# The same ends, spreading, maxima and first steps, with the conv's x added by VectorE behind the maxima

## The chip, the core and the metric

The kernel runs on one core of a Trainium2 chip. The core has five engines that work side by side, each through its own list of instructions in order: TensorE (PE in the profile; its weight loads are PEld), VectorE (DVE), ScalarE (ACT), GpSimd (POOL) and SyncE (SP), which here only issues DMAs. Engines wait for one another by semaphores. The metric is the time of one execution on the device, in microseconds (us); the median of several runs is compared. Everything is computed in float32.

## The reference

The input x has 16 images of 192 channels and 56 x 56 = 3136 pixels. Three layers of one kind and one of another follow, each with a residual:

```
x = x + rwkv(gn(x))          # layers 0, 1, 2
x = x + graph_conv(gn(x))    # layer 3

gn: per image and group of 6 channels, mean and variance over the group and all pixels

rwkv(x):                      # tokens t = the 3136 pixels, row by row
  k = x Wk,  v = x Wv,  r = x Wr
  forward and backward over the tokens, each with a decay per channel:
     y_t = (P_t + exp(u + k_t) v_t) / (Q_t + exp(u + k_t))
     P, Q: decaying sums of exp(k) v and exp(k) over the tokens before
  h = sigmoid(r) * (y_forward + y_backward) / 2
  h = layernorm over the 192 channels of each token
  return h Wo

graph_conv(x):
  m = max over the pixels 2 rows up, 2 rows down, 2 columns left and right (cyclic), minus x, and at least 0
  y = [x, m] (384 channels) times a matrix to 192 channels, + bias, batch norm
  return gelu(y)
```

## The kernel before

**Tiles.** The 16 images make 8 pairs. A pair's 2 x 192 channels lie as tiles of 128 partitions x 3 x 448 tokens: part j = 0 holds image A's first 128 channels, j = 2 image B's, and j = 1 the last 64 of both (A's in partitions 0-63, B's in 64-127; the code calls these halves LO and HI). A layer's tokens are cut into 7 chunks of 448 (8 image rows). Tiles live in a fixed set of slots in SBUF that go round a free list, results of matmuls in seven PSUM banks. What a layer hands to the next goes through DRAM.

**Runs and units.** A run is one layer of one pair. A forward unit "A" is one chunk of an RWKV layer: keys and values (`a_keys`, `a_values`), exp, forward scans (`a_q`, `a_p`), the bonus term (`a_den`, `a_num`) and y. A backward unit "B" is one chunk from last to first: gate r (`b_gate`, `b_exp`), backward scans (`b_q`, `b_p`, VectorE, L875), denominators (`b_den`, VectorE, L890), their inversion by Ln and Exp on ScalarE (`invert`, L975 and L978), numerators (`b_num`, L890), the mix of both directions with the gate (`b_mix`, nine GpSimd ops, L1031-L1033), squares (`b_squares`, ScalarE, L1040), sums over channels by matmuls with ones (`b_sums`, tile st, L1047-L1049), 1/deviation by `b_rs1` (ScalarE, L1055), `b_rs2` (PE) and `b_rs3` (ScalarE Ln and Exp, L1063 and L1065), the spreading of that row to all partitions by matmuls with a picking matrix (`b_spread`, tile rsb, L1071), scaling (`b_scale`, VectorE, L1076), output product (`b_out`, tile ops) and residual (`b_x`, L1089), then the sums that the next GroupNorm needs (`chunk_stats`, L734 and L735). A unit "C" is one chunk of the conv: maxima over rows and columns (`c_rows` L1114-L1116, `c_columns` L1125-L1129, VectorE), products of x and of the maxima (`c_product`, tile cv), gelu (`c_gelu`, ScalarE, L1150, with a load of its table before and of the usual one behind, L1155), and x added (`c_add`, GpSimd, L1159), then stores.

**GroupNorm** is folded into the weights: `norm_sums`, `norm_var` (mean nm, m2 = mean squared at L751, variance, rstd), `norm_fold` (weights times rstd on ScalarE, L770), and a mean column behind the first chunk (L765) that gives the bias through the same product.

**Order.** Even and odd pairs make two streams. A planner (L1207-L1242) lays out steps: a B turn has seven chunks, 6 to 0; the first stands alone (`backward_alone`), the other six stand beside six chunks of the other stream's next layer. There are 24 turns: 17 beside A, where chunk 5 runs in `both_a_first` and chunks 4 to 0 in `both_a`, and 7 beside C (`both_c`, 42 steps); what is left of the forward runs alone (`forward_a`, `forward_c`). At the end pair 6's last conv chunk and, after the step `neither`, pair 7's seven conv chunks stand alone. Within a step every engine's order is that in which the step's function calls the pieces, written out by hand; a piece enters its instructions at the end of the queues of all engines that it uses. `late` tells which B chunk still has which of its last stages to come; `gap()` marks places where a piece of the next run's norm may be put.

At the start, statistics of the first pair's input are counted for all seven chunks (`count`, ScalarE), before the first norm. A flag of checks on the values is reduced and written after the last chunk (L1758-L1763).

Of the kernel before, what the change touches and what calls it, by code (L numbers as in the profile page):

```python
# [473 lines left out]
def fast_path(ctx: ExitStack, tc: tile.TileContext, flag, x, wproj, wfold, wcfold, wconst, wgroup, sums, picks, vecs, out):  # L474
# [237 lines left out]
    class Run:  # L712
        def __init__(self, pr, l, stats, src=None, first=None):
            self.pr, self.l, self.stats, self.src = pr, l, stats, src
            self.xa, self.xb, self.xz = {}, {}, {}
            if first is not None:
                self.xa[0] = first
            self.begun, self.before = False, None
            self.bias, self.ps = {}, {}
            self.ek, self.ekv, self.h, self.den, self.sg, self.rs = {}, {}, {}, {}, {}, {}  # L720
            self.m, self.ml, self.q, self.p = {}, {}, {}, {}
            self.done = set()
# [23 lines left out]
    def norm_var(run):  # L746
# [4 lines left out]
        V.tensor_mul(m2, nm, nm)  # L751
# [10 lines left out]
        mean_column(run, run.xa[0])  # L762
# [47 lines left out]
    def load_weights(run):  # L810
        kv = wpool.tile([P, 2, FCOLS], F32, tag="kv", name=name("wkv"))
        if run.l == NLAYERS:
            nc.sync.dma_start(kv, wcfold)
            run.weights = kv, None
        else:
            nc.sync.dma_start(kv, wfold[run.l, :, 0:2, :])
            r = wpool.tile([P, 1, FCOLS], F32, tag="r", name=name("wr"))
            nc.sync.dma_start(r, wfold[run.l, :, 2:3, :])
            run.weights = kv, r
        load_ahead(("C" if run.l == NLAYERS else "A", run, 0))  # L820
# [14 lines left out]
    def load_ahead(unit):  # L835
# [7 lines left out]
        if kind == "C" and c not in run.xb:  # L843

            ring = run.xb[c] = Slot("m")
            nc.sync.dma_start(ring.t[:, :, 0:SHIFT], run.src[(c - 1) % NL][:, :, L - SHIFT : L])
            nc.sync.dma_start(ring.t[:, :, L - SHIFT : L], run.src[(c + 1) % NL][:, :, 0:SHIFT])
# [213 lines left out]
    def b_rs3(run, c):  # L1061
        rs, st = run.rs[c], run.ps["st"]
        S.activation(rs[HI, :], st[HI, :L], AF.Ln, bias=eps4[HI, :])  # L1063
        release(st)
        S.activation(rs[HI, :], rs[HI, :], AF.Exp, scale=-0.5)  # L1065

    def b_spread(run, c):
        rs = run.rs.pop(c)
        ps = run.ps["rsb"] = banks("rsb")
        for j, rows in ((0, slice(64, 96)), (2, slice(96, P)), (1, HI)):  # L1070
            PE.matmul(ps[j][:, :L], pick[rows, j, :], rs[rows, :], start=True, stop=True)  # L1071
# [36 lines left out]
    def c_rows(run, c):  # L1108
# [3 lines left out]
        if c == 0:  # L1112
            mean_column(run, m)
        V.tensor_max(m.t[:, :, SHIFT:E], xt[:, :, 0 : E - SHIFT], xt[:, :, 2 * SHIFT : L])  # L1114
        V.tensor_max(m.t[:, :, 0:SHIFT], m.t[:, :, 0:SHIFT], xt[:, :, SHIFT : 2 * SHIFT])
        V.tensor_max(m.t[:, :, E:L], xt[:, :, E - SHIFT : E], m.t[:, :, E:L])  # L1116

    def c_columns(run, c):
# [3 lines left out]
        for j in ORDER:  # L1122
            xr = xt[:, j, :].rearrange("p (r w) -> p r w", w=W)
            mr = ml.t[:, j, :].rearrange("p (r w) -> p r w", w=W)
            V.tensor_max(mr[:, :, 2 : W - 2], xr[:, :, 0 : W - 4], xr[:, :, 4:W])  # L1125
            V.tensor_max(mr[:, :, 0:2], xr[:, :, W - 2 : W], xr[:, :, 2:4])
            V.tensor_max(mr[:, :, W - 2 : W], xr[:, :, W - 4 : W - 2], xr[:, :, 0:2])
        V.tensor_max(ml.t, ml.t, xt)
        V.tensor_max(m, m, ml.t)  # L1129

    def c_product(run, c, half):
        n = L + 1 if c == 0 else L
# [7 lines left out]
    def c_gelu(run, c, more):  # L1140
        g, ps = run.ml[c], run.ps["c"]
        if c == 0:
# [14 lines left out]
    def c_add(run, c):  # L1157
        xs, g = run.xa.pop(c), run.ml.pop(c)
        G.tensor_add(g.t, g.t, xs.t)  # L1159
# [5 lines left out]
    def c_end(run, c, more):  # L1165
        c_gelu(run, c, more)
        c_add(run, c)

# [25 lines left out]
    for pr in range(npairs):  # L1194
        runs = [Run(pr, 0, None)]
        for l in range(NLAYERS):
            runs[-1].follow = Run(pr, l + 1, None)
            runs[-1].follow.before = runs[-1]
            runs[-1].dst = [dram.tile([P, 3, L], F32, tag=f"x{pr}_{l}_{c}", name=name("xd")) for c in range(NL)]
            runs.append(runs[-1].follow)  # L1200
# [11 lines left out]
    while ready[turn] is not None:  # L1212
# [16 lines left out]
        if len(streams) == 1 or ready[other] is None:  # L1229
# [8 lines left out]
            else:  # L1238
                ready[turn] = None
            steps += [[None, None, []]] + [[None, u, []] for u in units]  # L1240
# [139 lines left out]
    def both_a_first(b, a, nback, nfront, loads):  # L1380
# [7 lines left out]
        b_q(*b)  # L1388
        b_sigmoid(*b)
        b_p(*b)  # L1390
        b_den(*b)
        invert(b[0].ek[b[1]])
        b_num(*b)
# [3 lines left out]
        a_ekv(*a)  # L1397
# [4 lines left out]
        b_rs1(*l)  # L1402
        if nback is not None:
            b_exp(*nback[1:])
        a_q(*a)
        b_rs2(*l)
        b_rs3(*l)
        keys(nfront)
        a_p(*a)
        spread_and_scale(l)  # L1410
# [4 lines left out]
        b_sums(*b)  # L1415
        a_den(*a)
# [10 lines left out]
    def both_c(b, a, nback, nfront, loads):  # L1427
# [51 lines left out]
        gap()  # L1479
        b_num(*b)  # L1480
        b_sigmoid(*b)
        b_mix(*b)
        if ended:
            c_add(*ended)
# [33 lines left out]
    def forward_a(a, nback, nfront, nkeys, z):  # L1518
# [14 lines left out]
        if l:  # L1533
# [3 lines left out]
            b_spread(*l)  # L1537
            a_den(*a)
            invert(den())
            sum_up()  # L1540
            a_ekv(*a)
# [66 lines left out]
    def forward_c(a, nback, nfront):  # L1608
# [5 lines left out]
        if h and ahead and nfront[0] == "A":  # L1614
# [16 lines left out]
            return  # L1631
        c_product(*a, 0)
        c_rows(*a)
        c_columns(*a)
# [12 lines left out]
        c_end(*a, nfront is not None and nfront[0] == "C")  # L1647
# [23 lines left out]
    def backward_alone(b, nback, nfront):  # L1671
# [8 lines left out]
        invert(b[0].ek[b[1]])  # L1680
        b_sigmoid(*b)
        b_p(*b)
        gap(G)
# [22 lines left out]

    with tc.manual_schedule(engines={PE.engine, V.engine, S.engine, G.engine, nc.sync.engine}):
        S.preload_act_table_set(TABLES)
        first = chains[0][0]
        for c in range(NL):  # L1710
            load_ahead(("Z", first, c))
        for c in range(NL):
            count([(first, c, j) for j in ORDER], 3)
        for i, (b, f, z) in enumerate(steps):
# [32 lines left out]
            elif f:  # L1747
                forward_c(f[1:], nback, nfront)
# [7 lines left out]


    least = small.tile([P, 1], F32, tag="p2", name="fleast")  # L1758
    V.tensor_reduce(least, ok, mybir.AxisListType.X, ALU.min)
    ps = bank("psok")  # L1760

    PE.matmul(ps[0:32, 0:1], ones[:, 0, :], least, start=True, stop=True)
    V.tensor_scalar(flag, ps[0:1, 0:1], (P - 0.5) / C, None, ALU.is_lt)  # L1763
# [44 lines left out]
def _lay_out(inputs):  # L1808
# [24 lines left out]
    picks[64, 0, :] = picks[64, 1, 0:64] = picks[96, 1, 64:P] = picks[96, 2, :] = 1.0  # L1833
# [22 lines left out]
```

## Time and profile before

| what | us |
|---|---|
| median of 3 runs | 5122.39 |
| lowest and highest of them | 5105.55, 5124.11 |
| profiled execution, its own time | 5118.31 |
| its span (first to last instruction) | 5116.5 |
| busy: TensorE / VectorE | 4664.1 / 4769.5 |
| busy: ScalarE / GpSimd | 3690.8 / 2898.8 |
| mean granted TensorE clock | 0.95 of full |
| a turn beside A, from one turn's L890 `b_den` to the next turn's | about 179 |
| of it: step of chunk 5 / 4 / each of 3, 2, 1 | 30.5 or 32.1 / 25.7 / 23.6 |

A row of a group or of single instructions reads: line of the code, engine, operation, out<-in by tile names, shape; in brackets the idle time before it and what ended it. A row of a table by stretch reads: stretch and its length, then busy time of PE, PEld, DVE, ACT and POOL with the number of instructions, the granted clock, the share of DMA and GB/s.

### The profile page before, as it was taken

The page shows a single profiled execution, that of the slowest core. Times are in us where ns is not written, and L with a number is a line of the kernel's source. Part 1 is how long each engine was busy: PE and PEld are TensorE (multiplying, and loading weights), DVE is VectorE, ACT ScalarE, POOL GpSimd, SP SyncE. Part 2 cuts the span into 40 slices and gives each one's busy share as a digit, 9 for nine tenths or more (in the row PEclk, how much of TensorE's full clock was granted, in tenths as well). Part 3 has the DMA queues.
Part 4 walks back from the last instruction along what each step waited for, and adds up shares of the span by engine and source line. Part 5 has one row for each costly group of instructions (what it writes and reads, how often), then busy time and mean ns, then how long its engine had stood idle before and what let it go on. Part 6 is the DMA issues. An engine that isn't in the chain of part 4 may idle for free.

```text
span 5116.5 us, 51926 instructions
## 1 busy us (share of the span) xinstructions
PE 4664.1 (91%) x15542; PEld 1474.9 (29%) x15542; DVE 4769.5 (93%) x6275; ACT 3690.8 (72%) x7163; POOL 2898.8 (57%) x2247
## 2 busy tenths in 40 slices
PE   7899999999898999999989899999989999999897
PEld 3222222222222223222323222322222322223222
DVE  5999999998999999999899999999989999999995
ACT  6777777776767777777776777777767577777672
POOL 1656656654455666565455556666635466566562
PEclk9999999999899999999999999999999999999998
DMA  6122222234242222223424222222343322222233
GB/s 173 60 84 82 80 87 84 79 103 144 79 129 88 85 76 89 78 76 121 138 89 126 79 83 72 89 89 78 114 124 113 103 65 84 78 71 89 74 100 119
DMA packets 314276, 482.49 MB, mean 94 GB/s; under 512 B 66432, under 2 KB 306688, under 8 KB 313984
## 3 DMA queue, kind: packets, MB, share of 16 engines
q1 hardware_dynamic: 312832, 477.59, 29.2%
q8 instruction: 126, 2.06, 0.2%
q10 hardware_dynamic: 1152, 1.48, 0.1%
q14 instruction: 166, 1.36, 0.1%
HBM read 324.83 MB, written 154.14 MB: 94 GB/s over the span
## 4 chain that ended last, share of the span: by engine, by line
PE 35%; DVE 23%; POOL 18%; ACT 17%; issue 4%; DMA 2%; SPq 1%; POOLq 0%; DVEq 0%; ACTq 0%
POOL p L1033 6%; POOL p L1032 6%; POOL ekv L1031 5%; DVE p L875 5%; DVE q L875 4%; PE st L1049 3%; DVE q L890 2%; ACT sg L1003 2%; PE st L1059 2%; ACT sg L978 2%; ACT ek L978 2%; PE rsb L1071 2%; PE r L598 2%; PE r L605 2%; PE r L600 2%
## 5 line engine op out<-in xcount | busy, mean ns | idle before, releaser
L875 DVE TENSOR_TENSOR_SCAN q<-fdecays,ek 128x449 f32<-128x449 f32 (+1 forms) x1008 | 1023.5, 1068 | 12.8 <-ACT ek L920 10.3
L875 DVE TENSOR_TENSOR_SCAN p<-fdecays,ekv 128x449 f32<-128x449 f32 (+1 forms) x1008 | 1020.1, 1064 | 15.1 <-ACT ek L884 14.9
L1031 POOL TENSOR_TENSOR ekv<-ekv,ek 128x448 f32<-128x448 f32 x504 | 609.6, 1210 | 607.6 <-ACT ek L978 284.3
L982 POOL TENSOR_TENSOR p<-p,q 128x1344 f32<-128x1344 f32 x168 | 512.2, 3049 | 749.8 <-ACT q L978 468.6
L1033 POOL TENSOR_TENSOR p<-p,sg 128x448 f32<-128x448 f32 x504 | 616.8, 1224 | 83.4 <-ACT sg L978 34.0
L1032 POOL TENSOR_TENSOR p<-p,ekv 128x448 f32<-128x448 f32 x504 | 602.3, 1195 | 39.5
L886 POOL COPY ekv<-p 128x3 f32<-128x3 f32 x282 | 243.8, 864 | 567.0 <-DVE p L875 544.4
L920 ACT ACTIVATE ek<-k,k 128x448 f32<-128x448 f32 x504 | 297.1, 632 | 285.6 <-PE k L601 229.2
L1040 ACT ACTIVATE ek<-p 128x448 f32<-128x448 f32 x504 | 286.3, 572 | 231.2 <-POOL p L1033 230.8
L735 ACT ACTIVATE fjunk<-x 128x448 f32<-128x448 f32 x672 | 387.7, 577 | 37.6 <-DVE x L1089 11.1
L1071 PE MATMUL rsb<-rs,fpicks 32*128 32x448 f32 (+1 forms) x1008 | 355.3, 619 | 43.1 <-ACT rs L1065 43.1
L1076 DVE TENSOR_TENSOR p<-p,rsb 128x448 f32<-128x448 f32 x504 | 281.4, 611 | 103.7 <-PE rsb L1071 103.7
L890 DVE SCALAR_TENSOR_TENSOR ek<-ek,fcc,q 128x896 f32<-128x896 f32 x336 | 377.7, 1163 | 0.0
L734 ACT ACTIVATE fjunk<-x 128x448 f32<-128x448 f32 x600 | 343.5, 572 | 13.6
L1089 DVE SCALAR_TENSOR_TENSOR x<-ops,fwob,x 128x448 f32<-128x448 f32 x504 | 313.2, 669 | 29.5 <-PE ops L601 16.2
L890 DVE SCALAR_TENSOR_TENSOR q<-ek,fcc,q 128x896 f32<-128x896 f32 x336 | 334.7, 1035 | 6.3 <-ACT cvb L954 4.6
L940 DVE SCALAR_TENSOR_TENSOR ekv<-v,v,ek 128x448 f32<-128x448 f32 x504 | 312.3, 671 | 15.3 <-PE v L601 10.9
L890 DVE SCALAR_TENSOR_TENSOR ekv<-ekv,fcc,p 128x896 f32<-128x896 f32 x336 | 321.7, 997 | 0.0
L996 ACT ACTIVATE sg<-r,r 128x448 f32<-128x448 f32 x504 | 312.4, 626 | 10.2 <-PE r L607 8.3
L890 DVE SCALAR_TENSOR_TENSOR p<-ekv,fcc,p 128x896 f32<-128x896 f32 x336 | 293.6, 913 | 3.8 <-POOL ekv L886 1.7
L975 ACT ACTIVATE q<-q 128x1344 f32<-128x1344 f32 x168 | 221.5, 1318 | 96.9 <-DVE q L890 87.8
L598 PE MATMUL ops<-p,fwo 128*128 128x448 f32 x336 | 206.1, 700 | 84.5 <-DVE p L1076 84.5
(235 smaller groups left out, 11485.2 us busy)
## 6 DMA issues: line engine op xcount, KB each, us to landing
x<-xd SPq DMA_DIRECT2D x240, 672.0 KB, 5.3
xd<-x SPq DMA_DIRECT2D x168, 672.0 KB, 3.9
x<-in_x_dram SPq DMA_DIRECT2D x320, 224.0 KB, 4.5
x<-in_x_dram SPq DMA_DIRECT2D x320, 112.0 KB, 4.4
out_dram<-ml SPq DMA_DIRECT2D x112, 224.0 KB, 2.3
m<-xd SPq DMA_DIRECT2D x112, 168.0 KB, 5.2
wkv<-in_wfold_dram SPq DMA_DIRECT2D x24, 640.0 KB, 5.5
out_dram<-ml SPq DMA_DIRECT2D x112, 112.0 KB, 2.3
```

Source lines behind the costliest of these rows:

```text
L734: S.activation(junk, xt[:, j, :], AF.Identity, accum_out=stats[:, 0, j, c : c + 1])
L735: S.activation(junk, xt[:, j, :], AF.Square, accum_out=stats[:, 1, j, c : c + 1])
L875: V.tensor_tensor_scan(out, dec[:, column(j)].to_broadcast([P, L if first else L + 1]), e, 0.0, ALU.mult, ALU.add)
L890: by_channel(lambda js, i: V.scalar_tensor_tensor(dst.t[:, js, :], e.t[:, js, :], cc[:, i : i + 1], state.t[:, js, :], ALU.mult, ALU.add))
L940: V.scalar_tensor_tensor(e.t[:, j, :], ps[j][:, 0:L], b[:, j, :], run.ek[c].t[:, j, :], ALU.add, ALU.mult)
L982: G.tensor_mul(run.h[c].t, run.h[c].t, den.t)
L996: S.activation(sg.t[:, j, :], ps[j][:, 0:L], AF.Exp, bias=b[:, j, :], scale=-1.0, accum_out=run.chk[:, at : at + 1])
L1031: G.tensor_mul(y.t[:, j, :], y.t[:, j, :], den.t[:, j, :])
L1032: G.tensor_add(h.t[:, j, :], h.t[:, j, :], y.t[:, j, :])
L1033: G.tensor_mul(h.t[:, j, :], h.t[:, j, :], sg.t[:, j, :])
L1071: PE.matmul(ps[j][:, :L], pick[rows, j, :], rs[rows, :], start=True, stop=True)
L1089: V.scalar_tensor_tensor(xj, ps[j][:, 0:L], wob[:, column(j)], xj, ALU.add, ALU.add, accum_out=run.new[:, 0, j, c : c + 1] if c == 0 else ...
```

## The change

- Start: the first run's sums come from one VectorE reduction per chunk; ScalarE only squares.
- `norm_var`: m2 is made from the sums in PSUM and nm, instead of nm times nm.
- Spreading: `b_rs3` writes the same row with one more Exp into the lower 64 partitions too, and `b_spread` takes j = 1 from rows 0-63 instead of 64-127 (`picks` accordingly).
- Maxima: the two border operations of `c_rows` become one, the nine of `c_columns` three over all j.
- `both_a_first`: another order, in which the next B chunk's scans are done in this step, and 1/deviation and spreading of the chunk before follow right behind its sums.
- `both_c`: x is added to the gelu of the chunk before by VectorE, behind the maxima, not by GpSimd behind `b_mix`. That holds for five of a turn's seven chunks; the others stay on GpSimd.
- `forward_a`: `a_ekv` stands before `a_den`. `backward_alone`: a piece of the norm stands before the sigmoid and `b_p`, not behind.
- End: beside pair 6's last conv chunk the last B chunk's rest comes first, pair 7's last norm and maxima of two of its chunks are put there; pair 7's conv takes its chunks in the order 3, 4, 5, 2, 6, 1, 0, the flag is written before the last of them, and that one's gelu, addition (VectorE) and store go part by part.

The diff, cut to its core:

```diff
@@ Run, norm_var
+            self.c0 = 0
...
-        V.tensor_mul(m2, nm, nm)
+        V.scalar_tensor_tensor(m2, m[:, :, 0:1], -1.0 / T, nm, ALU.mult, ALU.mult)
...
-        mean_column(run, run.xa[0])
+        mean_column(run, run.xa[run.c0])
+        if run.c0 in run.m:
+            mean_column(run, run.m[run.c0])
@@ b_rs3, b_spread
+        S.activation(rs[LO, :], rs[HI, :], AF.Exp, scale=-0.5)
         S.activation(rs[HI, :], rs[HI, :], AF.Exp, scale=-0.5)
...
-        for j, rows in ((0, slice(64, 96)), (2, slice(96, P)), (1, HI)):
+        for j, rows in ((0, slice(64, 96)), (2, slice(96, P)), (1, LO)):
@@ c_rows, c_columns
-        V.tensor_max(m.t[:, :, 0:SHIFT], m.t[:, :, 0:SHIFT], xt[:, :, SHIFT : 2 * SHIFT])
-        V.tensor_max(m.t[:, :, E:L], xt[:, :, E - SHIFT : E], m.t[:, :, E:L])
+        mq, xq = (t.rearrange("p j (q k) -> p j q k", k=SHIFT) for t in (m.t, xt))
+        V.tensor_max(mq[:, :, ::3], mq[:, :, ::3], xq[:, :, 1:3])
...
-        for j in ORDER:
...
-            V.tensor_max(mr[:, :, 2 : W - 2], xr[:, :, 0 : W - 4], xr[:, :, 4:W])
-            V.tensor_max(mr[:, :, 0:2], xr[:, :, W - 2 : W], xr[:, :, 2:4])
-            V.tensor_max(mr[:, :, W - 2 : W], xr[:, :, W - 4 : W - 2], xr[:, :, 0:2])
+        xr, mr = (t.rearrange("p j (r w) -> p j r w", w=W) for t in (xt, ml.t))
+        V.tensor_max(mr[:, :, :, 2 : W - 2], xr[:, :, :, 0 : W - 4], xr[:, :, :, 4:W])
+        V.tensor_max(mr[:, :, :, 0:2], xr[:, :, :, W - 2 : W], xr[:, :, :, 2:4])
+        V.tensor_max(mr[:, :, :, W - 2 : W], xr[:, :, :, W - 4 : W - 2], xr[:, :, :, 0:2])
@@ c_add, c_end_in_parts
-    def c_add(run, c):
+    def c_add(run, c, eng=G):
         xs, g = run.xa.pop(c), run.ml.pop(c)
-        G.tensor_add(g.t, g.t, xs.t)
+        eng.tensor_add(g.t, g.t, xs.t)
...
+    def c_end_in_parts(run, c):
...
+        for j in ORDER:
+            S.activation(
+                g.t[:, j, :], ps[j][:, 0:L], AF.Gelu, bias=run.bias["c"][:, j, :], scale=conv_inv[:, column(j)]
+            )
+            release(ps[j])
+            V.tensor_add(g.t[:, j, :], g.t[:, j, :], xs.t[:, j, :])
+            if j == 1:
+                nc.sync.dma_start(out[b0, P:C, cols], g.t[LO, 1, :])
+                nc.sync.dma_start(out[b1, P:C, cols], g.t[HI, 1, :])
+            else:
+                nc.sync.dma_start(out[(b0, b1)[j // 2], 0:P, cols], g.t[:, j, :])
@@ planner
+            if units[0][0] == "C":
+                last = units[0][1]
+                last.c0 = 3
+                units = [("C", last, c) for c in (3, 4, 5, 2, 6, 1, 0)]
@@ both_a_first
         b_q(*b)
+        b_p(*b)
+        a_q(*a)
         b_sigmoid(*b)
-        b_p(*b)
         b_den(*b)
         invert(b[0].ek[b[1]])
+        a_ekv(*a)
         b_num(*b)
         b_mix(*b)
         for u in loads:
             load_ahead(u)
-        a_ekv(*a)
         b_squares(*l, (1,))
         if nback is not None:
             b_gate(*nback[1:])
         b_sums(*l)
         b_rs1(*l)
+        b_rs2(*l)
+        b_rs3(*l)
+        b_spread(*l)
         if nback is not None:
             b_exp(*nback[1:])
-        a_q(*a)
-        b_rs2(*l)
-        b_rs3(*l)
         keys(nfront)
         a_p(*a)
-        spread_and_scale(l)
+        if nback is not None:
+            b_q(*nback[1:])
+        b_scale(*l)
+        b_out(*l)
+        late[l] = 2
         b_squares(*b, (0,))
         a_save(*a)
         exp_keys(nfront)
         b_squares(*b, (2, 1))
         b_sums(*b)
+        if nback is not None:
+            b_p(*nback[1:])
         a_den(*a)
@@ both_c
         gap()
+        if ended:
+            c_add(*ended, V)
         b_num(*b)
         b_sigmoid(*b)
         b_mix(*b)
-        if ended:
-            c_add(*ended)
@@ forward_a
+            a_ekv(*a)
             a_den(*a)
             invert(den())
             sum_up()
-            a_ekv(*a)
@@ forward_c, beside pair 6's last chunk
+        if l0 and final:
...
+            b_squares(*l0)
+            c_product(*a, 0)
+            c_rows(*a)
+            c_columns(*a)
+            store()
+            b_sums(*l0)
...
+            b_rs1(*l0)
+            b_rs2(*l0)
+            b_rs3(*l0)
+            b_spread(*l0)
+            sum_up()
+            maxima(*r3)
+            b_scale(*l0)
+            b_out(*l0)
+            c_rows(*r4)
+            add(l0)
+            sum_up()
+            c_product(*a, 1)
+            gap()
+            gap()
+            c_columns(*r4)
+            gap()
+            gap()
+            c_gelu(*a, True)
+            c_add(*a)
+            return
...
+        if nfront is None:
+            flag_up()
+            c_end_in_parts(*a)
+            return
@@ backward_alone
         invert(b[0].ek[b[1]])
+        gap(G)
         b_sigmoid(*b)
         b_p(*b)
-        gap(G)
@@ main block
+        first.stats = input_stats()
         for c in range(NL):
-            count([(first, c, j) for j in ORDER], 3)
+            xs = first.xz.pop(c)
+            V.tensor_reduce(first.stats[:, 0, :, c : c + 1], xs.t, mybir.AxisListType.X, ALU.add)
+            chunk_stats(first.stats, xs.t, c, True)
+            xs.give()
@@ picks
-    picks[64, 0, :] = picks[64, 1, 0:64] = picks[96, 1, 64:P] = picks[96, 2, :] = 1.0
+    picks[64, 0, :] = picks[0, 1, 0:64] = picks[32, 1, 64:P] = picks[96, 2, :] = 1.0
```

## The prediction

> **What bounds the kernel now.** I read the page's engine rows, then its groups by line, then tables by stretch, then single instructions in order of time.
>
> ```profile
> PE 4664.1 (91%) x15542; PEld 1474.9 (29%) x15542; DVE 4769.5 (93%) x6275; ACT 3690.8 (72%) x7163; POOL 2898.8 (57%) x2247
> ```
>
> VectorE (DVE) and TensorE (PE) are both nearly full, so the stretch decides. Table by stretch (length, then busy time of PE, PEld, DVE, ACT, POOL, then granted clock):
>
> ```profile
> 21.00:55.00 34.00, 13.22 (x44) 8.26 (x44) 5.82 (x36) 27.79 (x85) 0.46 (x1) 1.00 1.07 258
> ...
> 594.75:618.35 23.60, 23.30 (x82) 7.14 (x81) 23.60 (x30) 19.25 (x37) 15.31 (x12) 1.00 0.25 88
> ...
> 4908.50:4931.70 23.20, 22.41 (x76) 6.78 (x76) 23.13 (x31) 18.79 (x35) 15.53 (x12) 1.00 0.42 133
> 4990.00:5030.00 40.00, 20.64 (x63) 6.94 (x64) 7.59 (x26) 17.85 (x44) 3.02 (x1) 0.71 0.23 76
> 5030.00:5104.00 74.00, 67.20 (x196) 21.75 (x196) 62.24 (x103) 15.82 (x23) 20.96 (x6) 0.93 0.49 150
> ```
>
> Row 1 is the start: ScalarE works, the others wait. Row 2 is one steady step of the 85 of B beside A: DVE has no gap, PE has 0.3 us, and a loop through three engines closes in the same time (below). Row 3 is a step of B beside the conv. Row 4 is the end's bare stretch (PE half idle, at clock 0.71), row 5 the last convs, on PE. The profiled execution's span is 5116.5 and its time 5118.3; my sum is against the latter, 4 us under the median of 5122.4.
>
> **Start.** Statistics are 40 Identity or Square passes on ScalarE from 21.5 to 49.5, 0.70 us apart; then VectorE:
>
> ```profile
> 49.51 0.20 DVE L740 TENSOR_REDUCE mv<-zstats 128x6 f32<-128x42 f32 x1 [16.32 <-ACT fjunk L735]
> ```
>
> The 21 Identity passes go, 21 × 0.70 = 14.7 us; VectorE's seven reductions of 1344 elements (1.6 us each, estimated from the 1.56 us of the two-input op of that size at L1128) fit its 16 us of idleness. The last chunk's load is issued at 21.4 and its kind takes about 5 us, so data are no bound before 27. **−14** (−8 if reductions and VectorE's setup work collide, −16).
>
> **End.** Now:
>
> ```profile
> 5012.31 1.15 DVE L1076 TENSOR_TENSOR p<-p,rsb 128x448 f32<-128x448 f32 x2 [22.79 <-PE rsb L1071]
> ...
> 5028.22 0.83 DVE L783 TENSOR_TENSOR wkv<-wkv 128x640 f32<-128x640 f32 x1 [1.84 <-DMA wkv<-in_wcfold_dram]
> ```
>
> ```profile
> 5058.98 3.35 POOL L1159 TENSOR_TENSOR ml<-ml,x 128x1344 f32<-128x1344 f32 x1 [14.01 <-ACT ml L1150]
> ...
> 5105.33 3.02 POOL L1159 TENSOR_TENSOR ml<-ml,x 128x1344 f32<-128x1344 f32 x1 [6.96 <-ACT ml L1150]
> ```
>
> The chain is: squares of the last chunk behind statistics on ScalarE (5003.97), rs1 5008.4, spread 5011.3, scale, product, residual add 5021.7, norm, folded weights, first conv product 5029.7; then seven convs of 9.0 us of PE with 6.7 us of idleness; last gelu 5105.2, GpSimd's add of 3.02, store issue to 5111.8, end 5116.5. With the squares in front of the statistics and the conv's weights no longer last, the first conv starts about 5009 (estimated by taking the 8.2 us of statistics, the 1.84 us wait and some 10 us of order out of the 5030). 7 × 9.0 + 3 us of remaining waits puts PE's end at 5075; the tail in parts (gelu 0.65, VectorE add 0.5–0.6, a store) is about 8 us instead of 12. End 5083: **−35** (−25 if the early maxima, 2 × about 5 us of VectorE, delay the norm; −45 if no waits are left).
>
> **Spreading: the added Exp.** b_rs3 issues one more ScalarE op per chunk, 168 in all; its row:
>
> ```profile
> L1065 ACT ACTIVATE rs<-rs x168: 572/573/575, 178.0 to 5010.6; 64x448 f32<-64x448 f32 x168
> ```
>
> Behind one another, such ops start 0.47 us apart. In the steady step there is a loop: st of PE ends 594.75, ScalarE's rs1, the forward denominators' inversion, the gate's exponents, rs3's Ln and Exp, the sigmoid, then the backward denominators' inversion to 606.0; nine GpSimd ops b_mix from 606.04 to 616.71; square, st, next rs1 at 618.37: 23.57 after the last rs1. The Exp sits in it, in front of L1003:
>
> ```profile
> 600.85 0.57 ACT L1065 ACTIVATE rs<-rs 64x448 f32<-64x448 f32 x1
> 601.45 1.33 ACT L1003 ACTIVATE sg<-sg 128x1344 f32<-128x1344 f32 x1
> ...
> 606.46 0.58 ACT L978 ACTIVATE ek<-ek 128x448 f32<-128x448 f32 x1
> ```
>
> As DVE's 23.58 is as long as the loop, the loop's slack is about 0.03 us a step: it becomes 24.0, so + 0.44 us in steady steps. What it buys is on PE:
>
> ```profile
> 604.59 1.97 PE L1071 MATMUL rsb<-rs,fpicks 32*128 32x448 f32 x6
> ```
>
> Six records; j = 0 and 2 (rows 64 and 96) share 0.95 us, j = 1 (64 rows, overlapping both) takes another 0.95. On rows 0–63 instead, j = 1 can run beside them: 1.0 us of PE less, 0.95 × 168 = 160 us of busy time, which counts only where PE is last. In steady steps it isn't. [...]
>
> **First steps of layers (17 turns).** A turn takes about 179 us: step 5 (both_a_first) 30.5 or 32.1, step 4 25.7, steps 3, 2, 1 23.6 each, the rest around step 0. VectorE's idle time is where the change aims:
>
> ```profile
> DVE p L1076 <- PE rsb L1071: 4.7, 2, 3.4
> DVE mv L740 <- ACT fjunk L735: 0.4, 1, 0.4
> ```
>
> (VectorE's waits of one turn, 509–690.) I placed the new order by hand on the rows of that turn: b_p and a_q come ahead of the sigmoid, the early fold lets keys start at 515.5 instead of 518.3, but sums of the previous chunk wait for the squares that stand behind the inversion, and the spread now waits for three ScalarE ops right behind rs1, with PE idle 1.8 us in front of it, since keys are queued behind it. st of the first chunk ends at 547.8 (was 547.7), b_scale of it at 558.8 (558.6): the wait moves from step 5 to step 4, and then three and a half steps each pay 0.44. Per turn +1.5 us (−5 if rsb's waits vanish, +3), less 0.27 for the a_ekv that forward_a now puts ahead of the bias wait: 17 × 1.2 = **+21** (−85 to +51).
>
> **Steps beside the conv (42).** L1114 now stands beside GpSimd's x add:
>
> ```profile
> 4908.56 3.71 DVE L1114 TENSOR_TENSOR m<-x 128x672 f32<-128x672 f32 x1
> 4912.20 0.49 DVE L1115 TENSOR_TENSOR m<-m,x 128x336 f32<-128x336 f32 x1
> 4912.61 0.49 DVE L1116 TENSOR_TENSOR m<-x,m 128x336 f32<-128x336 f32 x1
> ```
>
> Without a GpSimd op it takes 0.85 (at 5029.03). Over all chunks before 5030, L1114–L1116 lose 102 us so. The add itself, two-input, is 1.56 us on VectorE as L1128 is, 35 × 1.56 = 55 us; merging saves VectorE about 0.5 us a chunk (nine ops 2.13 us, three about 1.6). It waits for the gelu, which ends at 4939.7, some 2.5 us, and b_num is queued behind it, for which b_mix waits. But b_mix also waits for the sigmoid behind that gelu. The loop here measures 23.35 and with the Exp 23.8; the mean interval of b_mix over the five steps of a turn is 122.3/5 = 24.5. At 23.7 each a turn saves 3.6: 7 × 3.6 = **−25** (0 to −44). [...]
>
> **norm_var and the bare chunks.** With two SBUF inputs L751 is stretched in 13 of 32 cases:
>
> ```profile
> 1285.53 2.71 DVE L751 TENSOR_TENSOR m<-nm 128x3 f32<-128x3 f32 x1
> ```
>
> Alone it is 0.16. Reading PSUM as L753 does (0.16), six cases of 2.55 behind C turns, on a VectorE chain without gaps, give **−15** (0 if the chain is the loop's; −18). backward_alone's earlier fold is hidden by its stretched inversion; I cost it 0 (±3).
>
> **Sum.** 5118.3 − 14 − 35 + 21 − 25 − 15 = **5050**.
>
> **The rivals.** (1) *PE bounds first steps after all*: the rsb waits vanish there and the freed 0.95 us pulls the turn, 17 × −5 = −85 in place of +21: 4944. For it: 103.7 us of VectorE's waits are for rsb; against: PE waits for rs3 then. 0.15. (2) *The conv steps give nothing*: the add's wait for the gelu passes on to b_num and b_mix, C turns 0: 5075. For it: GpSimd idles 7.2 us there already, waiting for b_num; against: the sigmoid is late as well. 0.2. (3) *Slower*: the Exp is on the loop in every step, at its full 0.573 instead of the 0.44, 168 × 0.573 = +96, and conv and norm gains hide behind that loop; only start and end stay, 5118 − 49 + 96 = 5165. It decides as soon as the loop exceeds DVE's 23.58 and passes 49 us in all, that is 0.29 us a step. Against: outside the 85 steady steps VectorE waits elsewhere. 0.06. Between my forecast and that, the Exp at + 0.5 in half of them and a weak end: about 5110, 0.07. Forecast itself 0.52.
>
> **The numbers.** 5050, alone 5025–5072. The range for 8 in 10 leaves out (3), the case near 5110 and half of (1) (a turn 5 us shorter, or more): 4985 to 5100. This kernel's measurement tells 0.5%, 25.6 us, from no change. Faster by more (under 5097): 0.52 + 0.15 + 0.2 = 0.87, less 0.02 for tails: 0.85. Slower by more: 0.05. Between: 0.10.
>
> **What would show it.** Right: rsb's six records in about 1.0 us; steady steps of B beside A at 24.0 with VectorE waiting there for rsb; L1114's op at 0.85 in steps beside the conv, VectorE's add waiting about 2.5 us for the gelu and b_mix starts 23.7 apart; no m2 op over 0.2; first key product at 41; first of the last seven convs at about 5009 on the old clock, with 8 us behind PE's end. Wrong: steady steps at 23.6 (the Exp is hidden), turns under 175 us (rival 1), or conv steps at 24.5.

## The result and the profile after

The changed kernel takes 5187.1 us (median of 4 runs, 5185.34 to 5189.60) against 5120.9 (4 runs): ratio 1.0143, interval 1.0121 to 1.0164. It is **slower by 66 us**, where some 70 us less were forecast (5050). The profiled execution took 5185.34, its span is 5183.5.

The page's engine row after:

```profile
PE 4721.8 (91%) x15542; PEld 1500.5 (29%) x15542; DVE 4669.2 (90%) x5928; ACT 3767.0 (73%) x7286; POOL 2760.5 (53%) x2211
```

VectorE has lost 100 us of work and GpSimd 138, and yet the span is longer. TensorE runs the same 15542 matmuls and is busy 58 us longer: its matmuls have become slower, not more. The table by stretch after (a steady step of B beside A; the time ahead of the last seven convs; those convs):

```profile
607.44:631.61 24.17, 23.27 (x82) 7.12 (x80) 24.09 (x31) 19.82 (x39) 15.26 (x12) 1.00 0.25 86
5085.00:5110.00 25.00, 16.97 (x50) 6.40 (x48) 11.41 (x31) 11.40 (x27) 0.35 (x1) 0.70 0.24 84
5110.00:5174.00 64.00, 61.04 (x192) 19.77 (x190) 46.95 (x43) 14.17 (x21) 24.69 (x7) 1.00 0.52 156
```

The steady step has gone from 23.58 to 24.17. VectorE hardly waits in it (24.09 us busy, 0.08 us idle ahead of b_scale); most of what was added stands inside one of its operations, `a_den`, which took 1.72 us when it ran behind GpSimd's mix and takes 2.14 now that the mix's last operation (621.42 to 622.56) runs beside its start. Before and after:

```profile
616.88 1.72 DVE L890 SCALAR_TENSOR_TENSOR q<-ek,fcc,q 128x896 f32<-128x896 f32 x2
```

```profile
621.96 2.14 DVE L894 SCALAR_TENSOR_TENSOR q<-ek,fcc,q 128x896 f32<-128x896 f32 x2
```

To see where the rest went I cut each span at the first L890 operation of `b_den` (L894 after) of every turn. "Start" is what lies ahead of the first, "end" what lies behind the last; "last turn" is the last conv turn to its last b_den; the five columns add up to the span. They come from the one profiled execution of each kernel, the ratio from all of its runs: e1's profiled execution was the fastest of ten (5083.95, median 5095.83), e2's the slowest of ten (5128.19, median 5119.76), so a difference of a few us between two rows says little.

| kernel | start | 17 turns beside A | 6 conv turns | last turn | end | ratio to before, interval |
|---|---|---|---|---|---|---|
| before | 147.7 | 3052.8 | 1616.8 | 135.1 | 164.2 | 1 |
| changed | 135.9 | 3161.1 | 1612.8 | 134.3 | 139.3 | 1.0143 (1.0121-1.0164) |
| e1 first step old | 134.4 | 3060.6 | 1613.3 | 134.5 | 138.9 | 0.9971 (0.9961-0.9980) |
| e2 spreading old | 136.3 | 3126.0 | 1593.9 | 132.0 | 138.2 | 1.0018 (1.0005-1.0032) |
| e3 idle matmuls | 135.8 | 3117.0 | 1612.0 | 134.6 | 139.9 | 1.0075 (1.0056-1.0093) |
| e4 add on GpSimd | 132.0 | 3161.3 | 1628.8 | 135.3 | 140.0 | 1.0188 (1.0171-1.0205) |
| e5 spreading, 32 rows | 136.0 | 3160.9 | 1606.6 | 134.4 | 138.8 | 1.0151 (1.0135-1.0168) |
| e6 first step and spreading old | 136.3 | 3017.3 | 1578.1 | 132.8 | 137.9 | **0.9812** (0.9796-0.9829) |
| e7 keys first | 136.0 | 3089.5 | 1610.9 | 135.4 | 139.1 | 1.0006 (0.9993-1.0018) |
| e8 e7, spreading old | 136.1 | 3051.5 | 1580.5 | 132.7 | 138.1 | 0.9863 (0.9846-0.9879) |
| e9 Ln in PSUM | 131.8 | 3152.7 | 1609.6 | 134.3 | 138.4 | 1.0131 (1.0114-1.0148) |
| e10 before, new spreading | 147.2 | 3077.9 | 1635.6 | 136.7 | 166.0 | 1.0115 (1.0098-1.0132) |
| e11 e6, add on GpSimd | 137.4 | 3017.0 | 1597.1 | 133.1 | 140.4 | 0.9846 (0.9830-0.9863) |
| e12 e6, maxima unmerged | 136.6 | 3021.3 | 1581.2 | 132.4 | 143.2 | 0.9817 (0.9800-0.9833) |
| e13 e7, idle matmuls | 136.0 | 3074.7 | 1622.8 | 135.5 | 138.5 | 1.0005 (0.9995-1.0014) |
| e14 e13, spreading old | 134.9 | 3044.2 | 1584.1 | 132.7 | 137.6 | 0.9856 (0.9839-0.9872) |
| e15 64 outputs a matmul | 136.4 | 3135.2 | 1596.3 | 134.9 | 138.6 | a single run: 5143.3 us |
| e16 e1, 64 outputs | 131.5 | 3056.3 | 1595.2 | 134.9 | 139.5 | 0.9901 (0.9875-0.9927) |

So start and end gained 12 and 25 us, the seven conv turns 5, and the 17 turns beside A lost 108: 69 in the 13 that follow another one beside A, 39 in the other four, which stand first or behind a conv turn. Within a mean turn of the 13 the steps of chunks 6, 5 and 4 went from 13.4, 31.1, 25.7 to 16.3, 25.5, 32.6: together 4.1 us more; steps 3, 2, 1 cost 1.4 more. VectorE's waits of the third turn (b_den of chunk 6 to b_den of chunk 3) after:

```profile
DVE p L1082 <- PE rsb L1077: 9.1, 2, 8.5
DVE p L879 <- POOL p L1037: 2.2, 1, 2.2
DVE x L1095 <- PE ops L607: 0.4, 1, 0.4
```

The wait for rsb that the change aims at has moved one step on and become longer, 8.5 us. What TensorE does ahead of it, instruction by instruction:

```profile
529.18 0.92 PE L1053 MATMUL st<-p,fsums 128*32 128x448 f32 x4
531.32 0.95 PE L1053 MATMUL st<-ek,fsums 128*32 128x448 f32 x4 [1.21 <-ACT ek L1044]
532.90 0.96 PE L1063 MATMUL st<-rs,fpicks 64*64 64x448 f32 x2 [0.64 <-ACT rs L1059]
535.79 3.41 PE L1077 MATMUL rsb<-rs,fpicks 32*128 32x448 f32 x6 [1.93 <-ACT rs L1071]
539.13 1.86 PE L598 MATMUL k<-x,wkv 128*128 128x448 f32 x2
540.79 1.70 PE L599 MATMUL k<-x,wkv 128*128 128x448 f32 x2
...
543.66 1.02 PE L605 MATMUL k<-x,wkv 128*128 128x448 f32 x2
```

Three waits within 6 us (1.21, 0.64, 1.93), and then rsb takes 3.41 instead of 1.97 and a pair of key matmuls 1.86 instead of 1.02. The granted clock of the two kernels over the same stretch of that turn, before and after:

```profile
533.00:544.00 11.00, 10.34 (x38) 3.23 (x30) 7.62 (x11) 7.09 (x16) 8.83 (x10) 1.00 0.00 0
```

```profile
533.00:544.00 11.00, 9.07 (x17) 2.92 (x18) 8.10 (x10) 4.66 (x13) 8.87 (x9) 0.69 0.00 0
```

The third turn is no exception. From 24 to 38 us behind a turn's first b_den, the stretch with rsb and the keys, the granted clock is below 1.00 in all 17 turns of the changed kernel (0.55 to 0.88), and 1.00 in all 17 of the kernel before. The prediction had found the wait ahead of rsb (1.8 us there), and had counted the wait but not slower work behind it.

### The profile page after: what moved, and what is told of

The parts are those of the page before. It is cut to its first block, busy times and chain, and to the rows that moved or that the text cites. A ratio compares the mean times of both kernels' runs of the same rounds, so it can differ in the third digit from the quotient of the medians.

```text
span 5183.5 us, 51864 instructions
## 1 busy us (share of the span) xinstructions
PE 4721.8 (91%) x15542; PEld 1500.5 (29%) x15542; DVE 4669.2 (90%) x5928; ACT 3767.0 (73%) x7286; POOL 2760.5 (53%) x2211
## 4 chain that ended last, share of the span: by engine, by line
PE 43%; ACT 20%; POOL 15%; DVE 14%; issue 5%; DMA 1%; SPq 1%; DVEq 0%; POOLq 0%; ACTq 0%
POOL p L1037 5%; POOL p L1036 5%; POOL ekv L1035 5%; PE st L1053 4%; DVE p L879 3%; DVE q L879 3%; PE rsb L1077 3%; PE st L1063 2%; ACT ek L982 2%; ACT sg L982 2%; ACT sg L1007 2%; PE ops L598 2%; PE r L598 2%; PE ops L600 2%; ACT rs L1067 2%
## 5 line engine op out<-in xcount | busy, mean ns | idle before, releaser
L1036 POOL TENSOR_TENSOR p<-p,ekv 128x448 f32<-128x448 f32 x504 | 588.8, 1168 | 39.5
L890 POOL COPY ekv<-p 128x3 f32<-128x3 f32 x282 | 246.8, 875 | 463.7 <-DVE p L879 444.4
L1077 PE MATMUL rsb<-rs,fpicks 32*128 32x448 f32 (+1 forms) x1008 | 387.1, 650 | 94.8 <-ACT rs L1071 94.8
L737 ACT ACTIVATE fjunk<-x 128x448 f32<-128x448 f32 x672 | 387.6, 577 | 27.2 <-DVE x L1095 2.8
L894 DVE SCALAR_TENSOR_TENSOR ek<-ek,fcc,q 128x896 f32<-128x896 f32 x336 | 364.3, 1123 | 0.0
L736 ACT ACTIVATE fjunk<-x 128x448 f32<-128x448 f32 x579 | 331.4, 572 | 13.0
L894 DVE SCALAR_TENSOR_TENSOR q<-ek,fcc,q 128x896 f32<-128x896 f32 x336 | 335.5, 1038 | 1.7 <-ACT ek L888 1.7
L894 DVE SCALAR_TENSOR_TENSOR p<-ekv,fcc,p 128x896 f32<-128x896 f32 x336 | 296.1, 921 | 3.4 <-POOL ekv L890 1.7
L894 DVE SCALAR_TENSOR_TENSOR ekv<-ekv,fcc,p 128x896 f32<-128x896 f32 x336 | 291.5, 907 | 0.0
L979 ACT ACTIVATE ek<-ek 128x896 f32<-128x896 f32 (+1 forms) x253 | 237.3, 938 | 54.0 <-DVE ek L894 54.0
```

The lines of the kernel that those rows point to most:

```text
L736: S.activation(junk, xt[:, j, :], AF.Identity, accum_out=stats[:, 0, j, c : c + 1])
L737: S.activation(junk, xt[:, j, :], AF.Square, accum_out=stats[:, 1, j, c : c + 1])
L894: by_channel(lambda js, i: V.scalar_tensor_tensor(dst.t[:, js, :], e.t[:, js, :], cc[:, i : i + 1], state.t[:, js, :], ALU.mult, ALU.add))
L979: S.activation(s.t[:, js, :], s.t[:, js, :], AF.Ln)
L1036: G.tensor_add(h.t[:, j, :], h.t[:, j, :], y.t[:, j, :])
```

## The experiments

Each is an edit of the changed kernel unless it says otherwise; spans and turns are in the table.

**e1.** `both_a_first` in its old order, word for word.

> The changed kernel (5187) with the first step of a turn (both_a_first) in its old order, all else changed. Theory (clock): in the new order TensorE stands three times in that step (1.2, 0.6 and 1.9 us) and the granted clock drops (0.69 over 11 us in the changed kernel's third turn), so that the spreading and the key products behind it take 9.8 us instead of about 6.3; with the old order the drop goes, turns beside A come back from 184-187 to 180-182 (178-181 before, plus three to four steps of 0.57), and the total is 5100 to 5115. Rival (the added Exp is the main loss): turns stay at 184 or more, total 5165 or more.

Turns 3060.6, 100 us less than in the changed kernel; the total, 5095.8, is 4 us under the range of the theory. Over 512 to 533 us, its first step, the clock is whole:

```profile
512.00:533.00 21.00, 19.90 (x81) 5.68 (x80) 18.45 (x25) 13.31 (x23) 15.79 (x15) 1.00 0.00 1
```

From 24 to 38 us behind the first b_den it is 1.00 in all 17 turns. Most of the loss is the order of the first step. That the clock is its cause isn't shown by this, since the order changes with it.

**e2.** The three edits of the spreading undone (no Exp into LO, j = 1 from HI, picks).

> The changed kernel with the spreading as before: no Exp into the lower rows, j = 1 from rows 64-127. Theory: steady steps of B beside A go back from 24.15 to 23.58 (51 x 0.57 = 29 us), conv steps lose about 0.45 each (some 16 us), the clock drop in the first steps stays: total about 5140. If the wait for rs3, shorter by one Exp (1.93 to 1.46 us), is short enough to keep the clock: 5085. Rival (the Exp is hidden, steps are longer for another reason): within 10 us of 5187.

57 us of span come back (35 in the turns, 19 and 2 in the conv turns; steady steps 23.57); the median, 5119.8, lies between the first two cases. The Exp costs more than 45, and the clock still drops in the first step (0.69 over 531 to 542 us).

**e3.** Matmuls whose result is overwritten, in two of the three waits:

```diff
+    def idle(run, c, n):
+        for _ in range(n):
+            PE.matmul(run.ps["rsb"][0][0:32, :L], ones[:, 0, :], run.h[c].t[:, 0, :], start=True, stop=True)
...
+        l[0].ps["rsb"] = banks("rsb")
-        b_sums(*l)
+        b_sums(*l, 1)
         b_rs1(*l)
         b_rs2(*l)
+        idle(*l, 2)
         b_rs3(*l)
```

> The changed kernel with three matmuls of no use (ones with the scaled-to-be tile, 0.95 us each, into the banks that the spreading overwrites) in the waits of the first step: one ahead of the last part of the sums, two behind b_rs2. Order and dependences stay. Clock theory: the clock stays up, the spreading takes 2.0 instead of 3.4 us and the keys 4.3 instead of 6.4, VectorE's wait for rsb in the next step falls from 8.5 to about 5, turns lose 3.5 us: total about 5187 - 17 x 3.5 = 5127. Rival (the order itself makes the turns late, the clock is a side show): turns stay at 184 to 187, total 5180 to 5195.

Turns fall by 44 us, 2.6 a turn (3.5 expected; total 5143.1 instead of 5127), with more work on TensorE and the same order. The clock is below 1.00 in 2 of the 17 turns instead of 17. The same stretch of the third turn:

```profile
529.00:540.00 11.00, 10.69 (x32) 3.28 (x34) 7.97 (x11) 7.13 (x17) 8.52 (x9) 1.00 0.01 1
```

This shows the clock as a cause by itself, for 44 of the 100 us that the first step's order costs.

**e4.** `c_add` on GpSimd behind `b_mix`.

> The changed kernel with the conv's x added by GpSimd behind b_mix, as before. Theory (beside the conv the loop over ScalarE with its two table loads decides, so taking 50 us off VectorE there bought nothing): five conv steps of a turn sum to 122 to 125 (123.0 in the changed kernel), total 5175 to 5200. Rival 1 (VectorE's wait of 2.45 us for the gelu ahead of b_num is what costs): steps fall to 118, total about 5150. Rival 2 (GpSimd's add was the bound): steps rise by 1 each, total 5225.

Five conv steps stay at 122.7 as the theory has it, while the total, 5204.3, is 4 us over its range; the 16 us that the move is worth lie in the tails of the conv turns (131.1 to 133.8 a turn).

**e5, e15, e16.** The spreading cut finer: j = 1 in two matmuls of 32 rows by 64 outputs (e5); all of it in six such pieces (e15):

```diff
-        for j, rows in ((0, slice(64, 96)), (2, slice(96, P)), (1, LO)):
-            PE.matmul(ps[j][:, :L], pick[rows, j, :], rs[rows, :], start=True, stop=True)
+        for j, rows, to in ((0, slice(64, 96), LO), (2, slice(96, P), HI), (1, slice(0, 32), LO), (1, slice(32, 64), HI),
+                            (0, slice(64, 96), HI), (2, slice(96, P), LO)):
+            PE.matmul(ps[j][to, :L], pick[rows, j, to], rs[rows, :], start=True, stop=True)
```

> The changed kernel with j = 1 spread by two matmuls of 32 rows each (rows 0-31 to output partitions 0-63, rows 32-63 to 64-127) in place of one of 64 rows. In the changed kernel j = 1 still starts 0.95 us behind the other two, though its rows are its own. Theory (a tile of 64 rows doesn't run beside tiles of 32): now all four run together, the spreading takes 1.0 us in place of 1.97; steady steps stay at 24.15, since the loop and not TensorE is last; first steps gain up to 1 us each where VectorE waits for rsb: total 0 to 35 us under the changed kernel's 5187. Rival (a third matmul is never taken alongside): 1.97 us stays, or 2.9, and the total with it.

> The changed kernel with the spreading cut into six matmuls of 32 rows and 64 output partitions: four with rows of their own first (j = 0 to partitions 0-63, j = 2 to 64-127, both of j = 1), then the other halves of j = 0 and j = 2. Theory (what may run together is set by the outputs, 256 partitions' worth at a time): the first four start together, 1.0 us, then two more, 1.0. Rival (two at a time whatever their outputs): three pairs, 2.9 us.

Rows of the three kernels, changed, e5 and e15 (two records a matmul):

```profile
609.84 1.97 PE L1077 MATMUL rsb<-rs,fpicks 32*128 32x448 f32 x6
```

```profile
610.79 1.92 PE L1078 MATMUL rsb<-rs,fpicks 32*128 32x448 f32 x8
```

```profile
629.78 0.99 PE L1078 MATMUL rsb<-rs,fpicks 32*64 32x448 f32 x12
```

e5's pieces of j = 1 run as a pair behind the pair of j = 0 and 2, so its theory falls; in e15 all six run in 0.99 us, also the two pairs that share their rows, so both of its cases fall. In e15 all six have one form and none writes 128 partitions, and none starts late; which of the two made the difference stays open, since in the changed kernel (64 rows beside 32) and in e5 (64 outputs beside 128) the late pieces differ from the first pair in form too. In the old order of the first step (e16):

> The run with the first step's old order (ratio 0.9971), and the spreading cut into six matmuls of 32 rows by 64 output partitions, which ran all together in 1.0 us: the new spreading as it was meant, with the added Exp. Theory (the Exp costs 0.47 us a chunk on the chain, 80 us in all; the 0.95 us that TensorE saves come back only where VectorE or the loop wait for rsb, first steps and conv turns): 25 to 45 us less, ratio 0.988 to 0.992, still 35 us or more behind the old spreading in the same order (0.9812). Rival (with three at once the new spreading pays for its Exp): ratio 0.981 or less.

As expected in size: the spreading as it was meant gains 24 us of span on e1, 18 of them in conv turns (36 us by the ratios), and stays 55 us behind the old spreading (5057.5 against 5002.2; 46 by the ratios).

**e6.** e1's and e2's edits together.

> The changed kernel with both the first step's order and the spreading as before. What is left of the change: start, ends, maxima, m2, the conv's add, forward_a and backward_alone. From the turns of the two runs with one of them undone: turns beside A as before (179.7), six conv turns 3.9 us shorter each, start -12, end -25: total 60 to 65 us under the kernel before, ratio 0.987 to 0.989. Rival (the two undone parts were worth more together than apart, or the clock drops move elsewhere): ratio 0.993 or more.

5004.45 us, faster than both kernels, and by more than expected: with the Exp gone from e1, 79.6 us of span go (81 by the ratios), on average 0.47 for each of 168 chunks. A steady step of it is the kernel before's again, VectorE without a gap:

```profile
584.86:608.43 23.57, 23.26 (x82) 7.12 (x80) 23.57 (x31) 19.25 (x38) 15.31 (x12) 1.00 0.24 88
```

**e7, e8.** The next chunk's keys behind `b_rs2`, and the spreading behind `b_exp`, so that TensorE has work while ScalarE makes 1/deviation; e8 with the old spreading.

```diff
         b_rs2(*l)
+        keys(nfront)
         b_rs3(*l)
-        b_spread(*l)
         if nback is not None:
             b_exp(*nback[1:])
-        keys(nfront)
+        b_spread(*l)
```

> The changed kernel with the next chunk's key products put behind b_rs2, ahead of the spreading, so that TensorE has 4.3 us of work while ScalarE makes 1/deviation. Clock theory: no drop, and the keys no longer wait for the spreading: sums of the first chunk 4 us or more earlier, turns beside A 179 to 182, total 5090 to 5110. Rival (what is late is VectorE's or GpSimd's part of the new order): turns at 182.6 as with the matmuls of no use, total about 5143, or more.

> As the run before, and the spreading as before the change. Theory: the two gains add: steady steps 23.58, conv turns 3.2 us shorter than in the changed kernel, total 50 us under the run with the keys first alone, 5040 to 5060. Rival: the clock drops again somewhere in the first steps, as it did in the changed kernel with the spreading undone; then only 5080 to 5100.

72 of the 100 us come back by this order alone (total 5108.1, in the theory's range; e8's 5037.7 is 2 us under its own). 29 remain against e1, and in e7 the clock still drops behind the waits ahead of the keys, in the third turn:

```profile
522.00:532.00 10.00, 9.49 (x20) 2.83 (x20) 5.23 (x6) 6.73 (x17) 9.43 (x10) 0.66 0.01 2
```

But it does so in 8 of the 17 turns only. Twelve of them have the same two waits, about 1.2 us ahead of the last sums and 0.64 ahead of `b_rs2`; the clock falls in six of these and stays whole in the other six. The third and the fifth turn, 24 to 38 us behind their first b_den:

```profile
522.50:536.50 14.00, 13.99 (x32) 4.40 (x32) 9.02 (x11) 7.11 (x17) 9.01 (x9) 0.76 0.00 1
888.00:902.00 14.00, 14.00 (x54) 4.50 (x55) 11.08 (x14) 7.39 (x18) 10.59 (x11) 1.00 0.00 1
```

What tells these turns apart isn't shown.

**e13, e14.** e7 and e8 with three matmuls of no use in those waits.

> The run with the keys ahead of the spreading (ratio 1.0006), and three matmuls of no use in the two waits that it left: two ahead of the last part of the sums, one ahead of b_rs2. There the granted clock was still 0.66 over 522 to 532 us, and 29 us over the 17 turns remained against the old order. Theory (the clock is all that the new order costs): no drop in the first steps, the 17 turns fall from 3089.5 to 3055-3065 us, total 25 to 35 us less, ratio 0.994 to 0.996. Rival (scans put ahead of b_den make the sums late by themselves): turns at 3080 to 3090, ratio 0.999 or more.

> As the run before, and the spreading as before the change. Theory: 17 turns at 3010 to 3020, as with the old order (3017.3), ratio 0.979 to 0.983. Rival (the new order needs the clock and is late besides): turns at 3035 to 3050, ratio 0.986, as with the keys first and no such matmuls.

The clock is whole there (518 to 534 us: 1.00, and in all 17 turns), and the turns come down by 15 and 7 us, half and a fifth of what the theory wants; e13's ratio doesn't move and is the rival's (its profiled execution loses 12 us in its conv turns), e14's is the rival's too. Against the old order 14 us are left with the added Exp and 27 without it. So the order costs something besides the clock; which of its moves does isn't settled.

**e9.** The Ln of `b_rs3` written to its PSUM bank, both Exps reading it there.

> The changed kernel with b_rs3's Ln written back to its PSUM bank, and both Exps reading it there. In the changed kernel the second Exp overwrites what the first one reads and starts 0.61 us behind it (630.27, 630.88), not 0.47 as ops of that size do that don't touch one another. Theory (it waits for the first to end): now 0.47, steady steps 24.02 in place of 24.15, 168 x 0.13 = 22 us off, ratio 1.010. Rival (the size of the loop is set elsewhere): steady steps 24.15, ratio 1.0143.

The second Exp starts 0.55 behind the first (0.61 before), steady steps are 24.05, near the theory's 24.02. The interval of the ratio holds the rival's 1.0143 and not the theory's 1.010, so the 0.1 us a step isn't seen in the whole.

**e10.** The kernel before with the new spreading alone.

> The kernel before with the new spreading alone (one more Exp a chunk, j = 1 from rows 0-63). Theory, from the difference of the runs with the first step's old order with and without it (79.6 us of span): each of the 168 Exps stands whole on the chain, 0.47 to 0.6 us, ratio 1.015 to 1.020. Rival (as predicted: only steps that are bound by the loop pay, 0.44 in three and a half steps of 17 turns, and little beside the conv): +26 us, ratio 1.005 or less.

47 us of span, 59 by the ratio: between the two again. The 17 turns pay 25 us, as the prediction had it; the conv turns pay 19, which it didn't have as a loss.

**e11, e12.** e6 with the add on GpSimd, and with the maxima unmerged.

> The kernel with order and spreading as before (ratio 0.981), and the conv's x added by GpSimd again. Theory: the move to VectorE is worth what it was in the changed kernel, 16 us over six conv turns and their tails, so ratio 0.984 to 0.986, with the five conv steps of a turn at 119.6 to 122. Rival (without the added Exp VectorE is the bound beside the conv, and the stretched maxima cost in full): steps 122, tails longer too, ratio 0.990.

> The kernel with order and spreading as before (ratio 0.981), and the maxima unmerged. Theory: VectorE waits 1 to 2 us for the gelu behind the maxima in conv steps, which hides 0.5 us a chunk; only chunks that stand alone can lose: conv steps within 0.2 us in sum, total 0 to 8 us more, ratio 0.981 to 0.983. Rival: 56 chunks x 0.5 us = 28 us, ratio 0.9867.

Both as their theories had it. The move of the add is worth 19 us in six conv turns, again in their tails (steps 119.7 against 119.6). The merged maxima are worth 3 us there and 5 at the end; their ratio is not to be told from e6's.

## Why the prediction was wrong

**The step that failed is "First steps of layers": + 1.2 a turn, + 21 in all; measured + 108.** The order of the schedule by hand was right: the keys start at 514.9 (predicted 515.5), rsb waits for three ScalarE ops (1.93 us; 1.8), VectorE's wait moves to the step of chunk 4. But sums of the first chunk ended at 551.7 and not 547.8, and b_scale started at 562.6 and not 558.8. Of these 3.9 us, 3.3 are the matmuls of 535.8 to 543.2, which I placed at the durations that the kernel before has there at a granted clock of 1.00 (1.97, 1.02, 0.91, 0.64): rsb 1.4 us more, the first three pairs of key matmuls 0.8, 0.8 and 0.3. The trace of before held the warning: longer matmuls behind a wait (k at 55.1: 1.86 for two behind 2.77 us, 1.02 at 518.25), and a granted clock of 0.71 at the end, which I quoted. A nearer warning went unread: in the kernel before, the clock also falls, to 0.50 for 3.4 us, behind TensorE's wait for the folded weights (2.75 to 3.06 us) in five of the 13 turns beside A that follow another one, and those five are the ones whose step of chunk 5 took 32.1 and not 30.5, a difference that the prediction stated without a reason. Of the 100 us that the order costs, e3 gives back 44 by the clock alone, the keys' place 72 with part of the clock in it, and 14 to 27 stay with the order while the clock is whole; what of the order costs these stays open.

The + 108 are a balance: 100 for the order, 43 for the Exp (e1 to e6), and a gain of 36 that no term of the sum held (the turns of e6 are that much shorter than before). In the third turn of e6 the keys start 6.0 us behind the first b_den and not 9.15, TensorE waits 0.21 us for the folded weights and not 2.75, and the five drops behind that wait are gone. That points to the earlier fold in `backward_alone`, which the prediction costed at 0 (± 3); no run undoes it alone.

In the third turn the clock fell with no single wait over 2 us ahead of it: 3.8 of the 5.7 us from 530.1 to 535.8 were idle, in three pieces (1.21, 0.64, 1.93), and the granted clock was 0.50 over 536.2 to 543.0. Nor does the sum of waits decide alone: the same two waits in e7 were followed by a drop in six turns and by none in six.

**Spreading: mechanism right, size and place off.** The Exp is in the loop, as said, and steady steps pay for it: 0.57, not 0.44, since the two Exps and what is around them start 0.6 us apart and not 0.47. The prediction's own rows had that (L1065 at 600.85, the next op at 601.45). VectorE's wait for rsb in steady steps, named as a sign of being right, is 0.08 us in the step shown above; the added time stands in `a_den`. But I charged it to the turns only (26 us; e10: 25) and let conv steps keep their gain. Beside the conv the chain that ends last runs over ScalarE: rs1, rs3's Ln and both Exps, the gelu with its two table loads (1.28 us each), the gate's exponents, then TensorE. So the Exp is paid there in full, 0.58 us a step from e6 to e1, and as much again behind the steps (3.0 a turn), which the Exp's own length doesn't explain: 35 us in six conv turns. And TensorE's 0.95 us were not saved at all: that j = 1 runs beside the other two once its rows are its own was my estimate from the pair's row, and in the changed kernel it starts at 610.79, 0.95 us behind them.

**Conv steps and norm_var: − 40 predicted, − 5 measured, and − 41 in e6.** In the changed kernel the five steps of a turn stood at 24.5 each (122.7), the prediction's own sign of being wrong. Without the Exp the estimate holds, though not by its reason: the add as such changes the steps by nothing (e4, e11), nor do the merged maxima (e12); the add's 16 to 19 us lie behind the steps. What took the steps from 122.0 to 119.6 isn't shown. (The sum had a slip too: 122.3 less five times 23.7 is 3.8 a turn and 27 in all, not 3.6 and 25.) VectorE's wait for the gelu is there as said:

```profile
5055.94 1.56 DVE L1168 TENSOR_TENSOR ml<-ml,x 128x1344 f32<-128x1344 f32 x1 [2.42 <-ACT ml L1159]
```

Rival 2 had its sum right for the changed kernel (conv turns about 0), not its cause: the wait costs nothing that the steps show (119.6 with it in e6, 119.7 without in e11). m2 takes 0.16 us in all 32 places, as said.

**Start: − 14, measured − 12.** Sums are ready at 38.4 instead of 49.5, the first key product starts at 44.0 instead of 55.1 (41 was said):

```profile
38.39 0.20 DVE L742 TENSOR_REDUCE mv<-zstats 128x6 f32<-128x42 f32 x1
```

**End: − 35, measured − 25.** From the last b_den to the first conv product 61.0 us instead of 77.4 (20.7 less were predicted), the seven convs 68.3 instead of 74.6 (66), the tail 10.0 instead of 12.1 (8). What L1114 showed in the conv steps, 3.71 us beside GpSimd's add and 0.85 without it, is seen again here, where GpSimd's add of one chunk stands beside VectorE's maxima of the next:

```profile
5164.43 3.03 POOL L1168 TENSOR_TENSOR ml<-ml,x 128x1344 f32<-128x1344 f32 x1 [4.68 <-DVE ml L1132]
```

```profile
5164.47 4.41 DVE L1133 TENSOR_TENSOR m<-m,ml 128x1344 f32<-128x1344 f32 x1
```

4.41 instead of 1.56, and the last product of the maxima waits 0.84 us for it.

**The rivals.** (1) fell: with all matmuls of the spreading at once the 17 turns gain 4 us in the old order (e16) and 26 in the new one (e15), not 85. (3), the slower side, had the right mechanism in the Exp (80 us between e1 and e6, 96 said) and its price of 96 contained the 0.573 a chunk; but it took the first steps as safe, and the largest loss was in none of the cases. The chance of 0.05 for slower was too small because all cases took TensorE's durations as given.

## What to carry to other kernels

When an order by hand puts new waits in front of TensorE, price them twice: the wait, and the matmuls behind it, which here ran at a granted clock of 0.50 for 6.8 us of the third turn. Behind waits of 1.2 and 0.64 us the clock fell in 6 of 12 turns (e7), so a turn in which the clock held proves nothing for the next; look at all of them, and give the engine something that is ready (here the keys, 72 us). An operation that is added to save another engine's time must be set against the loop that it joins, in every stage: one ScalarE op of 0.57 us for each of 168 chunks cost 47 to 80 us of span and bought 24 at best (36 by the ratios). Undo the parts of a change one by one and together: start, ends, m2, maxima, the add and the reordered `forward_a` and `backward_alone` made 0.9812, and two other parts turned that into 1.0143.

## What the runs showed of the hardware

- Behind three waits of 1.21, 0.64 and 1.93 us within 6 us the granted clock was 0.69 over 11 us (changed, third turn); with three matmuls of no use in two of them it was 1.00 (e3). In the changed kernel it fell in all 17 first steps (0.55 to 0.88 over 24 to 38 us behind the first b_den; in some only the last two of these waits stood there), with those matmuls in 2 of 17.
- Behind two waits of 1.2 and 0.64 us (e7) the clock fell in 6 of 12 turns (0.76 over 14 us in the third, 1.00 in the fifth); behind a single one of 2.75 to 3.06 us (before) in 5 of 13 (0.50 for 3.4 us), behind one of 2.75 for instance and not behind one of 2.91. Neither the longest wait nor their sum told the turns apart.
- Two matmuls of 32 rows by 128 output partitions ran together, and a third of 64 rows (changed: 1.97 us for all), or two of 32 rows by 64 outputs (e5: 1.92), followed 0.95 us later although their rows were their own; six pieces of 32 rows by 64 outputs ran together, 0.99 us for all (e15), although two pairs of them shared their rows.
